# Two graph layers on one core: denominators taken up later, moved tiles and sums by ones re-dealt in the encoder, and another order at both ends of layer 1

## The chip, the cores and the metric

The kernel runs on one core of a Trainium2 chip. The metric is the device time of one execution in microseconds (us), and the median of three runs is given. The engines are PE (TensorE), ACT (ScalarE), DVE (VectorE), POOL (GpSimd) and SP (SyncE); PEld is the weight load of PE. Each works through its own instructions in order and waits for others by semaphores.

## The reference

4096 nodes with 512 features (4 heads of 128) and one adjacency `adj` of 4096 x 4096 (about 1% ones). Everything is float32.

```python
h = relu(layernorm(x)); x = x + layer0(h, adj); h = relu(layernorm(x)); x = x + layer1(h, adj)

# layer 0, per head: encoder attention, MLP, decoder attention with the same weights, MLP
Xw = h_head @ W;  f1, f2 = Xw . v1, Xw . v2
att = softmax over neighbours of sigmoid(f1_i + f2_j)
Xn = batchnorm(concat(att @ Xw))
emb = batchnorm(elu(Xn @ Wenc.T + b) + Xn)
Y = elu(concat((att @ emb_head) @ W.T))
out = batchnorm(elu(Y @ Wdec.T + b) + Y)

# layer 1, per head
feats = h @ W;  logits = leaky_relu(e_s_i + e_n_j, 0.2), neighbours only
out = relu(concat(softmax(logits) @ feats) + b)
```

## The kernel before, in words

All features lie transposed: partitions are features, columns are nodes. Five tiles `R` of 128 x 4096 hold one head each, or values of layer 1.

**Start.** Eight blocks of 512 nodes are loaded, normalized (statistics on DVE, three of four normalizations on DVE, the fourth on POOL), transposed on PE and multiplied with the heads' weights. Beside it POOL issues eight transfers (`copy_adjacency`, L446) that convert the adjacency from float32 to bytes in HBM, 1024 x 2048 each. Seven are issued here, the eighth in block 1 of the encoder (L545).

**Attention (L209 to L407)** is used three times: encoder, decoder, layer 1. Its outer loop runs over 8 blocks: 4 heads by 2 halves of 2048 target nodes. The inner loop has 32 steps j, one for each 128 source nodes. A step makes one tile `e` of 128 x 2048 weights: in the encoder and decoder two passes on ACT (L415 tanh, L416 exp) and one on DVE (L417, times the byte mask `a`, which SP loads); in layer 1 one pass on ACT (L785) and one on DVE (L786). Then PE multiplies it with the values in four products of 128 x 512 (L347), each in two instructions. Weight tiles come from rings of buffers: 8 in all in the encoder, 9 in layer 1. Every fifth tile of the encoder is stored by ACT's queue (L334) and loaded again in the decoder.

**Denominators.** The sums of the weights over all sources are made in three ways, listed by step in `ENC_FIRST`, `ENC` and `GAT` (L62 to L64) as a pair (moved, by ones). A *moved* tile is added by a DMA that POOL issues, into `acc2` or `w` (L359); each waits for the one before it. A tile *by ones* is multiplied with a block of ones on PE (L299) into one PSUM bank, `den`, which is the only one of its pool. All others are added by DVE into `acc` (L365, L367). At the end of a block PE adds both accumulators into `den` by ones.

**What follows a block** is done in the steps of the next one. `at(j, f)` puts a function at step j. At step 2 (`EVICT`) `ending` (L267) runs: ACT copies `den` to `dsb` (L246), POOL stores it and reads it back as a column `dcol` (L247, L249), and the four outputs are copied out of PSUM (DVE in the encoder L510, ACT in the others L621, L791). At step 7 DVE inverts the column (`invert_them`) and POOL stores the reciprocals `rinvs`. At steps 8, 9, 14 and 15 POOL spreads a piece over all partitions (`rb`, two buffers, L260), and five and six steps later the finishing functions run: times `rb` and statistics in the encoder (L514, L517), times `rb` and ELU in the decoder, times `rb`, ReLU and an accumulating store in layer 1 (L795, L798, L804). The decoder has no denominators of its own and reads the encoder's reciprocals. The last block of a stage finishes at once.

A scheduler builds each engine's order from the order in the code and its own estimates; `tc.issue_after(i)` and `pinned` put instructions behind a given one.

**Between.** `mlp_block` (L549) multiplies, applies ELU, adds the input and takes batch-norm coefficients (`bn_coefs`, L162) for each of four feature blocks. The decoder's MLP calls `residual` for the blocks already normalized. Layer 1 begins with the small products of `w1x` (L688, L689), then for each 512 nodes `centred` (mean by PE L700, difference L703, square L706, ReLU L707, sum of squares L708) and `deviation`; products with `w1x` follow (L731), scaled by ACT on the way out (L736). Before its attention the maximum of the scores is taken, exponentials are made, one row of terms is stored (`store_rows`, L771), and `ssum` is formed from `vacc` (L775, L776).

Of the kernel before, what the change touches and what calls it, by code (L numbers as in the profile page):

```python
# [31 lines left out]
FP = mybir.dt.float32  # L32
# [8 lines left out]
IB = 512  # L41
# [17 lines left out]
G_MAX = 75.0  # L59


ENC_FIRST = (), (4, 5, 10, 11, 15, 16, 20, 21, 25, 26, 30, 31)  # L62
ENC = (0, 3, 6, 9, 12, 15, 18, 21, 24), (4, 5, 13, 14, 30, 31)
GAT = (0, 2, 5, 7, 10, 12, 15, 17, 20, 22, 25), (9, 30, 31)  # L64

KEEP = 5
# [1 line left out]
EP = 2  # L68

EVICT = 2  # L70


VECS = [
# [6 lines left out]
def kernel(ctx, tc, x, xT, adjT, w0, w0T, v0, wencT, wdecT, vecs, w1, w1T, a1, outT):  # L80
# [12 lines left out]
    def nodes(r, ib):  # L93
        return r[:, ib * IB:(ib + 1) * IB]
# [4 lines left out]
    def bank():  # L99
        return psum.tile([P, IB], FP, name="ps")  # L100
# [13 lines left out]
    def vec_of(name):  # L114
        return vec[:, VECS.index(name), :]
# [46 lines left out]
    def bn_coefs(st, gamma, beta, a, b, lo, hi):  # L162

        mv = consts.tile([P, C, 2], FP, name="bmv", bufs=2)
        for fb in range(lo, hi):
            nc.vector.bn_aggr(mv[:, fb, :], st[:, fb].rearrange("p c s -> p (c s)"))
        a, b, mv = a[:, lo:hi], b[:, lo:hi], mv[:, lo:hi]
        rsqrt(a, mv[:, :, 1], BN_EPS)
        nc.vector.tensor_mul(a, a, vec_of(gamma)[:, lo:hi])
        nc.vector.tensor_mul(b, mv[:, :, 0], a)  # L170
        nc.vector.tensor_sub(b, vec_of(beta)[:, lo:hi], b)

    def heads_of(pv):

# [34 lines left out]
    def attention(what, keep, pools, weights, values, row_of, out, finish, ebufs, modes=None, invert=None,  # L209
# [53 lines left out]
        def at(j, f, *args):  # L263

            later.setdefault(j, []).append(lambda: f(*args))

        def ending(h, tb, po, den):  # L267

            dcol = denominators(h, tb, den) if den is not None else None
            outs = [out(spool, h, tb, s, po[s]) for s in range(SB)]  # L270
            if dcol is not None:
                at(EVICT + 5, invert_them, h, tb, dcol)
            rbs = {}
            for s, o in enumerate(outs):

                j = EVICT + 6 + s % 2 + s // 2 * 6
                at(j, lambda s=s: rbs.update({s: spread(h, tb, s)}))
                for k, f in enumerate(finish):
                    at(j + 5 + k, lambda f=f, s=s, o=o: f(spool, h, tb, s, o, rbs[s], False))

        def next_row_of(h, tb):
            rowb = keep.tile([P, TB], FP, name="rowb", bufs=2)
# [139 lines left out]
    with tc.tile_pool(name="keep", bufs=1) as keep:  # L422

        with tc.tile_pool(name="f_small", bufs=1) as small, tc.tile_pool(name="f_work", bufs=2) as work:
# [26 lines left out]
            for ib in range(NIB):  # L451
                st = work.tile([P, C, 6], FP, name="st")
                mv = work.tile([P, C, 2], FP, name="mv")
                for c in range(C):
                    nc.vector.bn_stats(st[:, c, :], xs[ib][:, c, :])
                for c in range(C):
                    nc.vector.bn_aggr(mv[:, c, :], st[:, c, :])
                rstd = work.tile([P, C], FP, name="rstd")
                last_dve = rsqrt(rstd, mv[:, :, 1], LN_EPS)
                hT = work.tile([P, C, IB], FP, name="hT")  # L460
                for c in range(C):
                    by_pool = c == C - 1
                    hn = work.tile([P, F], FP, name="hn", tag="hnp" if by_pool else "hn")
                    made = (nc.gpsimd if by_pool else nc.vector).tensor_scalar(
                        hn, xs[ib][:, c, :], mv[:, c, 0:1], rstd[:, c:c + 1], ALU.subtract, ALU.mult)

                    if by_pool and ib > 0:
                        with tc.issue_after(made.ins):
                            copy_adjacency(ib - 1, half_loaded)
                    pt = bank().rearrange("p (f n) -> p f n", n=P)  # L470
                    for fb in range(C):
                        last_pe = nc.tensor.transpose(pt[:, fb, :], hn[:, fb * P:(fb + 1) * P], ident)
                    last_act = nc.scalar.activation(hT[:, :, c * P:(c + 1) * P], pt, AF.Relu)
                if ib == 0:

                    pw = bank1()
                    with tc.issue_after(last_pe.ins):
                        for h in range(H):
                            nc.tensor.matmul(pw[:, 2 * h:2 * h + 2], w0Ts[:, h, :], v0s[:, h, :],
                                             start=True, stop=True)  # L480
                    pwh = pw[:, 0:2 * H].rearrange("p (h s) -> p h s", s=2)
                    with tc.issue_after(last_dve.ins):
                        nc.vector.tensor_copy(w0x[:, :, D], pwh[:, :, 0])
                        nc.vector.tensor_scalar_mul(w0x[:, :, D + 1], pwh[:, :, 1], 0.5)
                for c in range(C):
                    j = ib * C + c
                    for k in range(2):
                        pv = heads_of(bank())
                        for h in range(2):
                            nc.tensor.matmul(pv[:, h, :], hT[:, 2 * k + h, c * P:(c + 1) * P], w0x[:, 2 * k + h, :],  # L490
                                             start=True, stop=True)
                            nc.scalar.copy(block(R[2 * k + h], j), pv[:, h, 0:D])
                        nc.vector.tensor_copy(scores_of(j, k), pv[:, :, D:DX])
                if ib == SB - 1:
                    store_rows(rows[0], targets(0))
                    row0 = keep.tile([P, TB], FP, name="rowb", bufs=2)
                    row0_load = load_row(row0, rows[0], 0)
                    with tc.issue_after(row0_load.ins):
# [40 lines left out]
        with tc.tile_pool(name="enc", bufs=1) as spool:  # L539

            with tc.issue_after(last_act.ins), tc.issue_after(masks0[-1][1].ins):
                attention("enc", keep, spool, tanh_weights, R[0:4], lambda h, tb: (rows[tb], h), out_enc,
                          (scaled, statistics), 6, lambda n: ENC if n > 1 else ENC_FIRST, (TINY, ALU.max), "write",
                          row0=row0, masks0=masks0,
                          extras={(1, 12): lambda load: copy_adjacency(7, load),  # L545
                                  (2, 8): encoder_weights, (H * NTB - 1, NJ // 2): three_heads})


        def mlp_block(work, w, src, dst, gamma, beta, scale, between, early=None):  # L549
# [10 lines left out]
            for o in range(C):  # L560
# [7 lines left out]
                for ib in range(NIB):  # L568
# [18 lines left out]
                bn_coefs(stats, gamma, beta, a_mlp, b_mlp, o, o + 1)  # L587
# [50 lines left out]
    with tc.tile_pool(name="l_small", bufs=1) as small, tc.tile_pool(name="l_work", bufs=2) as work:  # L638
# [31 lines left out]
        def between(o, ib):  # L670
# [3 lines left out]
            elif o == C - 1 and ib >= NIB // 2:  # L674
                residual(o - 1, ib - NIB // 2)

        mlp_block(work, w, xd, x1, "dec_mlp_bn_gamma", "dec_mlp_bn_beta", None,
                  between)


# [4 lines left out]
        for fb in range(C):  # L685
            for h in range(H):
                k = 2 * (fb * H + h)
                nc.tensor.matmul(pw[:, k:k + 2], w1Ts[:, h, fb * P:(fb + 1) * P], a1s[:, h, :], start=True, stop=True)  # L688
        nc.vector.tensor_copy(w1x[:, :, :, D:DX], pw[:, 0:2 * C * H].rearrange("p (c h s) -> p c h s", h=H, s=2))  # L689
# [4 lines left out]
        def centred(ib):  # L694

            if ib >= NIB // 2:
                residual(C - 2, ib)
            residual(C - 1, ib)
            pm = bank()
            nc.tensor.matmul(pm, mean_of, S[ib], start=True, stop=True)  # L700
            hT = work.tile([P, C, IB], FP, name="hT")
            for fb in range(C):
                nc.vector.tensor_sub(hT[:, fb, :], nodes(x1[fb], ib), pm)  # L703
            sq = work.tile([P, C, IB], FP, name="sq", bufs=1)
            for fb in range(C):
                nc.scalar.activation(sq[:, fb, :], hT[:, fb, :], AF.Square)  # L706
                nc.scalar.activation(hT[:, fb, :], hT[:, fb, :], AF.Relu)  # L707
            nc.vector.tensor_reduce(S[ib], sq.rearrange("p c n -> p n c"), AX.X, ALU.add)  # L708
            return hT

# [47 lines left out]
        pm = bank1()  # L758
        nc.tensor.matmul(pm[:, 0:H], ones[0:H, :], mdiag, start=True, stop=True)
        nc.vector.tensor_copy(mbc, pm[:, 0:H])  # L760
        mb = mbc.unsqueeze(1).unsqueeze(3).to_broadcast([P, NTB, H, NJ // NTB])
        nc.vector.tensor_sub(jcol, score[:, 1], mb)
        nc.scalar.activation(jcol2, jcol, AF.Exp, scale=0.2)
# [95 lines left out]
```

## Time and profile before

| | |
|---|---|
| median of 3 runs | 3348.62 us (3343.92 to 3349.3) |
| profiled execution | 3349.09 us, its span 3347.3 us |
| granted PE clock | 0.99 |
| start, before the first full step | 0 to about 78 us |
| encoder attention, blocks 0 to 7 | about 78 to 1101 us |
| encoder MLP, decoder weights | about 1101 to 1250 us |
| decoder attention | about 1250 to 2138 us |
| decoder MLP | about 2138 to 2250 us |
| layer 1 features | about 2250 to 2399 us |
| layer 1 attention | about 2399 to 3347 us |
| DMA | 545.97 MB, 163 GB/s on average |

The profile is one execution; its times count from the first instruction. A line of the timeline gives start, duration, engine, line of the kernel, operation, output from input with shapes, and how many instructions are merged. What stands in brackets is how long the engine was idle before it and who released it. A line of the waits gives the waiting group, its releaser, the total in us, the times and the longest. "Landing" of a DMA is the time from its issue until its semaphore tells that all has arrived.

### The profile page before, as it was taken

The numbers are of one execution on the slowest core, as the hardware profiler recorded it, in microseconds if no ns is written. First come the engines' busy times: TensorE is split into PE (matmuls) and PEld (weight loads), VectorE is DVE, ScalarE is ACT, GpSimd is POOL, SyncE is SP. The second block draws the span as 40 slices with busy tenths as digits, with TensorE's granted clock in tenths as the row PEclk, the third lists the DMA queues.
The fourth block names the chain that finished last, engine by engine and source line by source line (L and its number), as shares of the span: only waits on it lengthen the run. The fifth ranks groups of instructions, "written<-read, shape, count | busy, mean of one in ns | idle before, by whom it ended". The sixth has DMA issues, their size and how long they took to land.

```text
span 3347.3 us, 26017 instructions
## 1 busy us (share of the span) xinstructions
PE 3239.2 (97%) x8943; PEld 1490.7 (45%) x8943; DVE 2679.2 (80%) x1912; ACT 2599.7 (78%) x1908; POOL 321.9 (10%) x466
## 2 busy tenths in 40 slices
PE   7998999999999999999999999999899999999999
PEld 6333434433434464444444444448644444444443
DVE  6898889889889765556665666586599999999999
ACT  7988899999999438999999999566656665665554
POOL 2000100100100000000000000024201111101110
PEclk9999999999999999999999999999999999999999
DMA  9984867867867003434443443232288789878876
GB/s 204 195 169 142 231 188 220 228 185 222 231 192 197 28 32 123 144 120 148 142 147 114 150 151 123 75 119 90 72 203 208 187 203 217 200 178 194 217 179 156
DMA packets 178437, 545.97 MB, mean 163 GB/s; under 512 B 20164, under 2 KB 23492, under 8 KB 144000
## 3 DMA queue, kind: packets, MB, share of 16 engines
q0 software_dynamic: 41360, 197.51, 30.7%
q1 hardware_dynamic: 126288, 293.66, 25.8%
q10 hardware_dynamic: 10656, 53.15, 3.9%
q8 instruction: 70, 1.15, 0.1%
q14 instruction: 63, 0.52, 0.0%
HBM read 378.15 MB, written 95.82 MB: 142 GB/s over the span
## 4 chain that ended last, share of the span: by engine, by line
PE 46%; DVE 24%; issue 12%; ACT 9%; DMA 8%; DVEq 0%; ACTq 0%; POOL 0%; POOLq 0%
PE ps L347 31%; DVE e L786 8%; PE ps L557 7%; DVE e L417 6%; DVE R L367 6%; ACT e L415 5%; PE ps L731 3%; DMA w<-e 3%; ACT e L416 3%; DVE acc L367 2%; DMA rb<-rinvs 2%; DMA a<-mask 2%; PE den L299 1%; PE ps L490 1%; PE ps L612 1%
## 5 line engine op out<-in xcount | busy, mean ns | idle before, releaser
L347 PE MATMUL ps<-e,R 128*128 128x512 f32 x6048 | 2643.6, 597 | 71.9 <-DVE e L417 54.9
L347 PEld LDWEIGHTS ps<-e,R 128*128 128x128 f32 x6048 | 1144.0, 191 | 1562.7 <-issue 1405.0
L417 DVE TENSOR_TENSOR e<-e,a 128x2048 f32<-128x2048 f32 (+1 forms) x470 | 1052.6, 2260 | 426.0 <-ACT e L416 404.1
L415 ACT ACTIVATE e<-rowb,score 128x2048 f32<-128x2048 f32 (+1 forms) x470 | 912.7, 1968 | 95.2 <-PE ps L347 59.0
L416 ACT ACTIVATE e<-e 128x2048 f32<-128x2048 f32 (+1 forms) x470 | 871.4, 1880 | 16.4 <-DVE e L417 10.0
L785 ACT ACTIVATE e<-rowb,nq,jcol 128x2048 f32<-128x2048 f32 x224 | 455.9, 2085 | 196.3 <-DMA w<-e 110.8
L786 DVE SCALAR_TENSOR_TENSOR e<-e,jcol,a 128x2048 f32<-128x2048 f32 (+1 forms) x259 | 590.6, 2317 | 3.7 <-ACT e L785 3.7
L367 DVE TENSOR_TENSOR R<-R,e 128x2048 f32<-128x2048 f32 x128 | 291.6, 2278 | 0.0
L367 DVE TENSOR_TENSOR acc<-acc,e 128x2048 f32<-128x2048 f32 x126 | 287.9, 2285 | 2.1
L557 PE MATMUL ps<-R,w 128*128 128x512 f32 x512 | 220.3, 592 | 0.6 <-DVE w L524 0.6
L260 POOL DMA_DIRECT2D rb<-rinvs x88 | 54.6, 652 | 1135.2 <-DVE R L514 834.5
L557 PEld LDWEIGHTS ps<-R,w 128*128 128x128 f32 x512 | 97.2, 190 | 122.7 <-issue 117.7
L359 POOL DMA_DIRECT2D w<-e x77 | 64.9, 843 | 620.7 <-DVE e L786 255.5
L731 PE MATMUL ps<-w1x,hT 128*128 128x260 f32 x512 | 117.8, 389 | 2.8 <-ACT hT L707 2.8
L577 ACT ACTIVATE ex<-ps,bias 128x512 f32<-128x512 f32 x64 | 44.0, 687 | 95.6 <-PE ps L557 78.5
L798 ACT ACTIVATE R<-R,vec 128x512 f32<-128x512 f32 x32 | 23.1, 720 | 117.3 <-DVE R L795 116.8
L731 PEld LDWEIGHTS ps<-w1x,hT 128*128 128x128 f32 x512 | 97.9, 193 | 22.8 <-ACT hT L707 4.4
L359 POOL DMA_DIRECT2D acc<-e x54 | 45.7, 846 | 635.5 <-DVE e L417 340.0
L785 ACT ACTIVATE e<-w,nq,jcol 128x2048 f32<-128x2048 f32 (+1 forms) x35 | 65.5, 1937 | 31.6 <-DMA dacc<-e 29.0
L299 PE MATMUL den<-e,ones 128*32 128x512 f32 x680 | 82.5, 599 | 0.0
L579 DVE SCALAR_TENSOR_TENSOR ex<-ex,re 128x512 f32<-128x512 f32 x64 | 44.9, 701 | 35.7 <-ACT re L578 35.7
L736 ACT ACTIVATE R<-ps,rstd 128x128 f32<-128x128 f32 x128 | 38.5, 366 | 40.4 <-PE ps L731 39.5
(158 smaller groups left out, 1269.8 us busy)
## 6 DMA issues: line engine op xcount, KB each, us to landing
a<-mask SPq DMA_DIRECT2D x720, 256.0 KB, 3.2
w<-e POOLq DMA_DIRECT2D x77, 1024.0 KB, 8.1
acc<-e POOLq DMA_DIRECT2D x54, 1024.0 KB, 8.5
ekeep<-e ACTq DMA_DIRECT2D x48, 1024.0 KB, 8.5
e<-ekeep SPq DMA_DIRECT2D x48, 1024.0 KB, 4.8
rb<-rinvs POOLq DMA_DIRECT2D x88, 256.0 KB, 5.2
mask<-in_adjT POOLq DMA_DIRECT2D x8, 2048.0 KB, 75.2
rowb<-rows SPq DMA_DIRECT2D x16, 1024.0 KB, 6.5
```

Of the source, the lines that this page charges most:

```text
L260: nc.gpsimd.dma_start(rb, everywhere(rinvs[h][tb], 0, s * IB, IB))
L299: last_ones = nc.tensor.matmul(den[s * 32:(s + 1) * 32, :], ones[:, 0:32], t[:, s * IB:(s + 1) * IB], start=not begun, stop=stop)
L347: last_main = nc.tensor.matmul(b, block(values[h], j), e[:, s * IB:(s + 1) * IB], start=(j == 0), stop=(j == NJ - 1))
L359: nc.gpsimd.dma_start(sums2 if n else dacc, e, **({"accum_op": ALU.add} if j > moved[0] else {}))
L367: nc.vector.tensor_add(acc, acc, e)
L415: nc.scalar.activation(e, rowb, AF.Tanh, bias=column(score[:, 1], j, h), scale=0.5)
L416: last_act = nc.scalar.activation(e, e, AF.Exp, scale=0.5)
L417: last_dve = nc.vector.tensor_mul(e, e, a)
L557: nc.tensor.matmul(z, w[:, fb, o * P:(o + 1) * P], nodes(src[fb], ib), start=(fb == 0), stop=(fb == C - 1))
L731: nc.tensor.matmul(b[:, 0:2 * DX], hT[:, fb, c * P:(c + 1) * P], w1x[:, fb, 2 * k:2 * k + 2, :].rearrange("p h x -> p (h x)"), start=(fb = ...
L785: last_act = nc.scalar.activation(e, rowb, AF.Relu, bias=column(nq, j, h), scale=column(jcol, j, h))
L786: last_dve = nc.vector.scalar_tensor_tensor(e, e, column(jcol2, j, h), a, ALU.add, ALU.mult)
```

## The change

The copy of `den`, its store and its column move from step 2 to step 4 (`INVERT`), while the outputs are still evicted at step 2. The inversion moves from step 7 to 10, the spreading from 8, 9, 14, 15 to 11, 12, 18, 19, and the finishing functions follow six and seven steps after. The lists change: the encoder's blocks 2 to 7 have eleven moved tiles (nine before) and four by ones (six before); its first two blocks keep twelve by ones, the first pair one step later. The eighth conversion of the adjacency is issued at the start, behind the seventh. At the start the statistics of the second 512 nodes stand behind the normalizations of the first. At the entry of layer 1 the copy of `w1x`'s added columns stands behind the last coefficients of the MLP; the difference is written to `sq`, ReLU reads it there, and the square is taken in place. Before layer 1's attention the sums for `ssum` stand ahead of the exponentials, and the row is stored after them.

```diff
-ENC_FIRST = (), (4, 5, 10, 11, 15, 16, 20, 21, 25, 26, 30, 31)
-ENC = (0, 3, 6, 9, 12, 15, 18, 21, 24), (4, 5, 13, 14, 30, 31)
+ENC_FIRST = (), (5, 6, 10, 11, 15, 16, 20, 21, 25, 26, 30, 31)
+ENC = (0, 2, 5, 7, 10, 12, 15, 17, 20, 22, 25), (8, 9, 30, 31)
 GAT = (0, 2, 5, 7, 10, 12, 15, 17, 20, 22, 25), (9, 30, 31)
...
 EVICT = 2
+INVERT = 4
...
-            dcol = denominators(h, tb, den) if den is not None else None
             outs = [out(spool, h, tb, s, po[s]) for s in range(SB)]
-            if dcol is not None:
-                at(EVICT + 5, invert_them, h, tb, dcol)
+            if den is not None:
+                def invert_later():
+                    dcol = denominators(h, tb, den)
+                    at(INVERT + 6, invert_them, h, tb, dcol)
+
+                at(INVERT, invert_later)
...
-                j = EVICT + 6 + s % 2 + s // 2 * 6
+                j = INVERT + 7 + s % 2 + s // 2 * 7
                 at(j, lambda s=s: rbs.update({s: spread(h, tb, s)}))
                 for k, f in enumerate(finish):
-                    at(j + 5 + k, lambda f=f, s=s, o=o: f(spool, h, tb, s, o, rbs[s], False))
+                    at(j + 6 + k, lambda f=f, s=s, o=o: f(spool, h, tb, s, o, rbs[s], False))
...
-                for c in range(C):
-                    nc.vector.bn_stats(st[:, c, :], xs[ib][:, c, :])
+
+                with pinned([first_hn] if ib == 1 else []):
+                    for c in range(C):
+                        nc.vector.bn_stats(st[:, c, :], xs[ib][:, c, :])
...
+                    if ib == 0 and not by_pool:
+                        first_hn = made
...
                             copy_adjacency(ib - 1, half_loaded)
+                            if ib == NIB - 1:
+                                copy_adjacency(ib, half_loaded)
...
-                          extras={(1, 12): lambda load: copy_adjacency(7, load),
-                                  (2, 8): encoder_weights, (H * NTB - 1, NJ // 2): three_heads})
+                          extras={(2, 8): encoder_weights, (H * NTB - 1, NJ // 2): three_heads})
...
-        nc.vector.tensor_copy(w1x[:, :, :, D:DX], pw[:, 0:2 * C * H].rearrange("p (c h s) -> p c h s", h=H, s=2))
+        with tc.issue_after(last_coefs.ins):
+            nc.vector.tensor_copy(w1x[:, :, :, D:DX], pw[:, 0:2 * C * H].rearrange("p (c h s) -> p c h s", h=H, s=2))
...
+            sq = work.tile([P, C, IB], FP, name="sq", bufs=1)
+            for fb in range(C):
+                nc.vector.tensor_sub(sq[:, fb, :], nodes(x1[fb], ib), pm)
             hT = work.tile([P, C, IB], FP, name="hT")
             for fb in range(C):
-                nc.vector.tensor_sub(hT[:, fb, :], nodes(x1[fb], ib), pm)
-            sq = work.tile([P, C, IB], FP, name="sq", bufs=1)
+                nc.scalar.activation(hT[:, fb, :], sq[:, fb, :], AF.Relu)
             for fb in range(C):
-                nc.scalar.activation(sq[:, fb, :], hT[:, fb, :], AF.Square)
-                nc.scalar.activation(hT[:, fb, :], hT[:, fb, :], AF.Relu)
+                nc.scalar.activation(sq[:, fb, :], sq[:, fb, :], AF.Square)
...
+        pss = bank1()
+        for h in range(H):
+            last_sum = nc.tensor.matmul(pss[:, h:h + 1], vacc[:, h, :], ones[:, 0:1], start=True, stop=True)
+        nc.vector.tensor_scalar_mul(ssum, pss[:, 0:H], TINY)
         mb = mbc.unsqueeze(1).unsqueeze(3).to_broadcast([P, NTB, H, NJ // NTB])
...
-        store_rows(rowsg, g.rearrange("p t h q -> p (t h q)"))
-
-        pss = bank1()
-        for h in range(H):
-            nc.tensor.matmul(pss[:, h:h + 1], vacc[:, h, :], ones[:, 0:1], start=True, stop=True)
-        nc.vector.tensor_scalar_mul(ssum, pss[:, 0:H], TINY)
+        with tc.issue_after(last_sum.ins):
+            store_rows(rowsg, g.rearrange("p t h q -> p (t h q)"))
```

More of the change, by code (lines that the diff above doesn't have):

```diff
@@ L170, in bn_coefs @@
         nc.vector.tensor_mul(b, mv[:, :, 0], a)
-        nc.vector.tensor_sub(b, vec_of(beta)[:, lo:hi], b)
+        return nc.vector.tensor_sub(b, vec_of(beta)[:, lo:hi], b)
     def heads_of(pv):
@@ L586, in mlp_block @@
                     between(o, ib)
-                bn_coefs(stats, gamma, beta, a_mlp, b_mlp, o, o + 1)
+                last = bn_coefs(stats, gamma, beta, a_mlp, b_mlp, o, o + 1)
+            return last
         with tc.tile_pool(name="m_small", bufs=1) as small, tc.tile_pool(name="m_work", bufs=3) as work:
@@ L675, in between @@
                 residual(o - 1, ib - NIB // 2)
-        mlp_block(work, w, xd, x1, "dec_mlp_bn_gamma", "dec_mlp_bn_beta", None,
+        last_coefs = mlp_block(work, w, xd, x1, "dec_mlp_bn_gamma", "dec_mlp_bn_beta", None,
                   between)
```

## The prediction

> **What bounds the kernel now.** First the busy shares and the span. TensorE looks full, but only the decoder (1250 to 2140 us) runs at its pace: 109.87 us a block of 256 products. The list of waits (us in total, times, longest) shows what stands in front of the others.
>
> ```profile
> span 3347.3 us, 26017 instructions
> PE 3239.2 (97%) x8943; PEld 1490.7 (45%) x8943; DVE 2679.2 (80%) x1912; ACT 2599.7 (78%) x1908; POOL 321.9 (10%) x466
> ```
>
> ```profile
> ACT dsb L246 <- PE den L299: 44.9, 7, 11.2
> ...
> DVE R L795 <- DMA rb<-rinvs: 29.5, 6, 6.7
> ...
> DVE R L514 <- DMA rb<-rinvs: 13.0, 3, 11.9
> ```
>
> Then the timelines of single engines give each wait its place. In the **encoder** ScalarE binds:
>
> ```profile
> 714.03 3.88 ACT L415 ACTIVATE e<-rowb,score 128x2048 f32<-128x2048 f32 x2
> 722.86 0.58 ACT L246 COPY dsb<-den 128x512 f32<-128x512 f32 x1 [4.94 <-PE den L299]
> 723.34 3.71 ACT L416 ACTIVATE e<-e 128x2048 f32<-128x2048 f32 x2
> ```
>
> Its copy of the denominators waits 4.94 us for TensorE's sums, with two exponentials behind it. In the stretch 594.9 to 719.2 ACT is busy 119.22 of 124.3 us: the wait is nearly all its idle time. In the **second encoder block**:
>
> ```profile
> 233.50 0.78 POOL L446 DMA_DIRECT2D mask<-in_adjT  x1
> 234.97 1.08 POOL L260 DMA_DIRECT2D rb<-rinvs  x2 [0.69 <-DMA rinvs<-dcol]
> ...
> 264.53 0.69 DVE L514 TENSOR_TENSOR R<-R,rb 128x512 f32<-128x512 f32 x1 [11.86 <-DMA rb<-rinvs]
> ```
>
> The reciprocals stand in Pool's queue behind the 8th conversion of the adjacency and land 29.6 us after their issue; VectorE stands 11.86 us. In **layer 1's attention** VectorE stops each block for the same kind of transfer:
>
> ```profile
> 3024.97 0.69 DVE L795 TENSOR_TENSOR R<-R,rb 128x512 f32<-128x512 f32 x1 [6.66 <-DMA rb<-rinvs]
> 3143.72 0.69 DVE L795 TENSOR_TENSOR R<-R,rb 128x512 f32<-128x512 f32 x1 [6.23 <-DMA rb<-rinvs]
> ```
>
> TensorE is near its floor there (109.87 plus five sums of 0.905 = 114.4 us). From the timeline of TensorE the blocks end 114.8, 114.9, 115.4, 117.0, 119.1, 118.7 us apart. At the **entry of layer 1** a copy stands in front of the last MLP step:
>
> ```profile
> 2251.63 0.19 DVE L689 COPY w1x<-den 128x32 f32<-128x32 f32 x1 [2.29 <-PE den L688]
> ```
>
> **What the Trainium skill says.** "PSUM — Partial Sum Buffer", Engine vs sequencer instructions: the queues of ScalarE, VectorE and GpSimd are strict FIFO. The trace agrees: the exponentials start at 723.34, after the copy. "DMA: Bandwidth & Descriptors", Issuing engines are not separate DMA queues: transfers of all issuers interleave on the same 16 engines. The trace agrees: stores of kept weights land in 4 to 5 us alone and 9 to 11 beside an accumulation, which takes 10 to 11 instead of about 8. "Perfetto Trace Analysis", Identifying the Most-Contended Engine: matmul busy share is a poor measure for TensorE; here it is 97% while blocks differ by 15 us.
>
> **The change, part by part.** Orders are those of the two built programs. The base is the profiled execution: 3349.1 us, span 3347.3 plus 1.8 around it; the median is 0.5 lower.
>
> *1. Denominators later, encoder blocks 2 to 7.* In ScalarE's built order the copy passes not two steps but two exponentials (1.80 us each, 3.60). The wait before, as a sum: DVE's last idle time is at tile 15 (773.44). From there to tile 30 it has 16 masks of 2.21, 11 adds of 2.255, 4 small operations of 0.605, together 62.5; then 0.35 for hand-overs, two tiles of products (6.87) and four sums (3.62): 73.4. ACT has 19 tanh of 1.895 and 18 exponentials of 1.80, 68.4. The difference, 4.95, is the traced 4.94. After: multiplying and statistics move from tiles 12-20 to 16-25, so more lies after DVE's last idle, now tile 13: 18 masks, 12 adds, 8 small ones, 71.6, plus 10.84, against 21 tanh and 22 exponentials, 79.4. That leaves 3.0 of wait: 1.9 less a block, six blocks, **-11.4**. Bounds: the wait wholly gone, -29; nothing, 0. Two sums less on TensorE (1.8 us a block) lie under ScalarE; they would count only if TensorE were late. VectorE's adds stay at 16. What is late next is the same copy.
>
> *2. Eleven moved tiles.* Two more accumulations a block are issued by Pool. Each waits for the one before; Pool's other issues wait behind. They hold their tile until they land; ACT asks for the same buffer 8 tiles later, some 29.6 us. A tile is masked 6 to 14 us after ACT starts it, a landing takes 4.5/8.5/12.6 us (min/median/max), so a backlog of some 5 us is covered. Moved tiles now come every 2.5 tiles of 3.73, 9.3 us, close to the mean landing of 9.5 (without the first of a block). I take 0; bounds -0.5 a block (DMA tails) and the first rival.
>
> *3. Eighth conversion at once, block 1.* The 11.86 wait goes, and 1.3 of small VectorE idles (0.57, 0.69) with ScalarE's earlier release. But the seventh conversion lands at 212.0 (issue 55.8 plus 156.2), the eighth then some 27 to 30 later, 239 to 242, and now the denominators queue behind it: two small transfers of about 3.2 each less overlap, 245. VectorE is at the inversion about 242.5 (208.5, four copies 2.4, six adds 13.5, eight masks 17.7, plus gaps): 2.5 lost. Mask loads in that stretch share the engines: VectorE lost 1.75, 1.28 and 1.43 between 183 and 206; I take 1.5. **-9**; bounds -13 and -4.
>
> *4. Start.* The third normalization no longer waits behind two statistics that wait for their input (2.24 idle); TensorE's gap of 2.78 shrinks. Block 0 is then paced by mask loads that land in 15 to 22 us, so little of it lasts: **-1**, bounds -2.7 and +0.5.
>
> *5. Entry of layer 1.* The copy goes behind the coefficients: -2.2 (the 2.29 wait). ReLU before squares brings the first weights forward, and the sums of squares come 1 us later: **-3** together, bounds -4.5 and -1.5. *Exit:* ssum's wait moves ahead of the row's store; ScalarE lost 2.53 to it, but VectorE now waits 1.8 for the sum before the row's terms; 0, bounds -1 and +1.6.
>
> *6. Layer 1's attention.* ScalarE's and Pool's order around the denominators is the same as before; only the first multiplication moves from after tile 13 to after tile 16: three masks of 2.27 and two adds of 2.25, 11.3 us later, more than the longest wait of 6.7. The waits go; TensorE gets back 0.6+2.2+4.3+3.9 over 114.8, and about 1 in the last block: **-12**. VectorE's idle 29.5 isn't the gain, since TensorE's queue covered the rest. Next late: TensorE itself. Bounds -13 and -4 (third and fourth reciprocals now behind more accumulations).
>
> *7. Decoder.* Its finishing steps and the order of kept-weight loads move, but TensorE idles 2.6 of 890 us: 0; if the cover went, one late step of 3.4 a block.
>
> Sum: 11.4+9+1+3+12 = 36.4, so 3349.1-36.4 = **3312.7**.
>
> **Rivals.** *Tiles held by moved sums.* For it: layer 1 has the same positions, and ACT waits there 110.8 us for such landings; it has slack, the encoder has none. Against: 9.5 is just within. At landings of 10.1 the seven accumulations after tile 10 fall 5 us behind by tile 22, ACT waits 4 to 5 a block, 3.0 of which the copy's wait gives back: the 11.4 are gone and a few us more. 3313+15 = 3328.
> *Slower.* The same queue as the bound: ten accumulations a block make each further us of landing cost 8 to 10. It decides when a block takes 129, 7 us over my 121.8 (6 x 7 = 43 eats the 36.4 and 6.7 more), at landings near 11; at 11.3, 131: 3368. Against: accumulations follow one another, so two more don't overlap; mean landings in layer 1, at 80% DMA share, are 8.4.
> *The wait goes wholly.* -29 for -11.4: 3295. Against: the sum in 1.
> *Reciprocals late again in layer 1*: gain 4 instead of 12: 3321.
> *Nothing comes of it*: the waits return one step later: 3345.
>
> **How the numbers follow.** Likeliest 0.56; tiles held 0.17; wholly gone 0.12; late reciprocals 0.08; slower 0.04; nothing 0.03. A difference of 0.2% (6.7 us) is about what can be told from none. Faster 0.93, same 0.03, slower 0.04. The range 3297 to 3336 takes in the likeliest, late reciprocals, most of the tiles held and half of the wholly gone.
>
> **What would show it.** ACT's wait at the copy near 3 us, encoder blocks 122 apart; ACT waiting for accumulations in the encoder speaks for the first rival. No VectorE wait on reciprocals in layer 1, blocks 114.8 apart; block 1 near 129 with a short wait at the inversion; the products of layer 1 three us earlier after the MLP. I am wrong if encoder blocks stay at 124 or VectorE waits for reciprocals.

## The result and the profile after

| | before | after |
|---|---|---|
| median | 3347.14 us (3343.92 to 3349.3, 4 runs) | 3310.01 us (3307.08 to 3313.2, 4 runs) |
| profiled execution, its span | 3347.3 us | 3308.6 us |

The change makes the kernel faster: ratio 0.989, 95% interval 0.9873 to 0.9907. The forecast was 3312.7. The profiled spans differ by 38.7 us; each stage's share comes from TensorE's timelines. A block is counted from the end of TensorE's sums of one block to that of the next, the decoder MLP from its first product.

| stage | forecast | measured |
|---|---|---|
| start and encoder block 0 | -1 | -5.4 |
| encoder block 1 (137.87, then 133.15) | -9 | -4.7 |
| encoder blocks 2 to 7 (752.3, then 733.4) | -11.4 | -18.9 |
| encoder MLP and decoder | 0 | -1.7 |
| decoder MLP to layer 1's first sums (382.63, then 381.95) | -3 | -0.7 |
| layer 1's attention from there (826.6, then 819.2) | -12 | -7.4 |
| sum | -36.4 | -38.7 |

The total was met, its terms were not: two were too small, three too large, and the decoder's is scatter (see below). First two lines of the page of the kernel after, then its list of waits (us in total, times, longest).

```profile
span 3308.6 us, 25868 instructions
...
PE 3226.6 (98%) x8847; PEld 1492.2 (45%) x8847; DVE 2677.1 (81%) x1912; ACT 2602.9 (79%) x1908; POOL 329.1 (10%) x478
```

```profile
ACT dsb L247 <- PE den L303: 19.6, 7, 5.2
...
DVE R L808 <- DMA rb<-rinvs: 14.3, 4, 8.7
...
DVE dcol L254 <- DMA dcol<-dens: 6.3, 1, 6.3
...
DVE R L524 <- DMA rb<-rinvs: 1.1, 2, 0.8
```

Busy times have hardly moved: what went are waits. The copy's 44.9 became 19.6, layer 1's 29.5 became 14.3, the 13.0 at L514 (11.86 of them in the second encoder block) became 1.1, and one is new, for `dcol`. Steady blocks of the encoder show it, one before and then two neighbours after (us, then busy time and instructions of PE, PEld, DVE, ACT and POOL, then granted clock, DMA share, GB/s):

```profile
722.79:846.87 124.08, 118.94 (x322) 49.75 (x321) 114.23 (x62) 119.22 (x65) 11.54 (x17) 1.00 0.75 212
```

```profile
701.76:823.86 122.10, 118.39 (x305) 50.09 (x305) 115.61 (x63) 119.22 (x65) 13.18 (x19) 0.99 0.85 233
823.86:944.68 120.82, 118.39 (x305) 50.05 (x305) 113.20 (x65) 119.21 (x65) 13.16 (x19) 0.99 0.89 244
```

ScalarE is busy for the same 119.22 us; its idle time shrinks. From its timeline after:

```profile
817.48 3.70 ACT L420 ACTIVATE e<-e 128x2048 f32<-128x2048 f32 x2
823.92 0.59 ACT L247 COPY dsb<-den 128x512 f32<-128x512 f32 x1 [2.75 <-PE den L303]
824.41 3.90 ACT L419 ACTIVATE e<-rowb,score 128x2048 f32<-128x2048 f32 x2
```

The wait is 2.75 where it was 4.94. It alternates with 1.48 from block to block, and so does the order that the scheduler built for VectorE at the end of a block. Blocks 2 to 6 are 120.8, 122.1, 120.8, 122.1 and 120.8 apart. In the second encoder block (block 1), from the timelines of Pool, VectorE and TensorE:

```profile
206.08 0.59 POOL L248 DMA_DIRECT2D dens<-dsb  x1 [151.85 <-ACT dsb L247]
241.84 0.59 POOL L250 DMA_DIRECT2D dcol<-dens  x1 [35.17 <-DMA dens<-dsb]
```

```profile
244.26 0.17 DVE L254 TENSOR_SCALAR dcol<-dcol 128x16 f32<-128x16 f32 x1 [6.30 <-DMA dcol<-dens]
```

```profile
239.61 3.60 PE L351 MATMUL ps<-e,R 128*128 128x512 f32 x8
249.00 9.43 PE L351 MATMUL ps<-e,R 128*128 128x512 f32 x16 [5.79 <-DVE e L421]
```

An 8 KB store stands 35 us behind the 8th conversion, which landed at 240.8. VectorE stands 6.30 us for the column that depends on the store, and TensorE 5.79 us for VectorE. In layer 1 VectorE still waits four times for reciprocals, the longest time in the third block:

```profile
2657.27 0.69 DVE L808 TENSOR_TENSOR R<-R,rb 128x512 f32<-128x512 f32 x1 [8.73 <-DMA rb<-rinvs]
```

That block takes 118.88 and the fourth 115.54 (its wait is 3.05). The other full ones take 114.83 and the last 111.39. At the entry of layer 1 the copy follows the coefficients without a wait:

```profile
2222.37 0.16 DVE L172 TENSOR_TENSOR coefs<-vec,coefs 128x1 f32<-128x1 f32 x1
2222.45 0.18 DVE L700 COPY w1x<-den 128x32 f32<-128x32 f32 x1
```

### The profile page after: what moved, and what is told of

Same layout as the page of the kernel before. It is cut to its first block, busy times and chain, and to the rows that moved or that the text cites. A ratio compares the mean times of both kernels' runs of the same rounds, so it can differ in the third digit from the quotient of the medians.

```text
span 3308.6 us, 25868 instructions
## 1 busy us (share of the span) xinstructions
PE 3226.6 (98%) x8847; PEld 1492.2 (45%) x8847; DVE 2677.1 (81%) x1912; ACT 2602.9 (79%) x1908; POOL 329.1 (10%) x478
## 4 chain that ended last, share of the span: by engine, by line
PE 67%; DVE 16%; issue 9%; ACT 5%; DMA 3%; DVEq 0%; ACTq 0%; POOL 0%; POOLq 0%
PE ps L351 52%; PE ps L566 7%; DVE e L421 4%; DVE e L799 4%; DVE R L371 4%; PE ps L743 3%; ACT e L419 2%; PE den L303 2%; DVE acc L371 2%; ACT e L420 2%; DMA a<-mask 2%; PE ps L622 1%; PE ps L348 1%; PE ps L500 1%; DMA rb<-rinvs 1%
## 5 line engine op out<-in xcount | busy, mean ns | idle before, releaser
L363 POOL DMA_DIRECT2D w<-e x77 | 64.6, 839 | 643.6 <-DMA w<-e 267.5
L743 PE MATMUL ps<-w1x,hT 128*128 128x260 f32 x512 | 119.6, 393 | 1.8 <-ACT hT L717 1.8
L363 POOL DMA_DIRECT2D acc<-e x66 | 55.6, 842 | 607.7 <-DMA acc<-e 225.7
L588 DVE SCALAR_TENSOR_TENSOR ex<-ex,re 128x512 f32<-128x512 f32 x64 | 45.0, 703 | 35.7 <-ACT re L587 35.5
L303 PE MATMUL den<-e,ones 128*32 128x512 f32 x584 | 70.9, 599 | 0.0
```

Of the source, the lines that this page charges most:

```text
L303: last_ones = nc.tensor.matmul(den[s * 32:(s + 1) * 32, :], ones[:, 0:32], t[:, s * IB:(s + 1) * IB], start=not begun, stop=stop)
L363: nc.gpsimd.dma_start(sums2 if n else dacc, e, **({"accum_op": ALU.add} if j > moved[0] else {}))
L743: nc.tensor.matmul(b[:, 0:2 * DX], hT[:, fb, c * P:(c + 1) * P], w1x[:, fb, 2 * k:2 * k + 2, :].rearrange("p h x -> p (h x)"), start=(fb = ...
```

## The experiments

The ratio is to the kernel before, timed beside each. "Theory" is what I held before a run, after the traces that I had by then; "rival" is the other account. Several theories fell.

| kernel | median us | ratio to before (95%) |
|---|---|---|
| later_alone | 3317.07 | 0.9905 (0.9889 to 0.9922) |
| lists_alone | 3347.83 | 0.9995 (0.9987 to 1.0004) |
| lists_old | 3315.08 | 0.9896 (0.9882 to 0.9909) |
| cast_back | 3306.2 | 0.987 (0.9856 to 0.9883) |
| cols_other_queue | 3301.08 | 0.9852 (0.9839 to 0.9866) |
| start_old | 3307.47 | 0.9876 (0.986 to 0.9891) |
| gat_inv5 | 3304.92 | 0.9862 (0.9848 to 0.9875) |
| edges_old | 3311.91 | 0.9883 (0.987 to 0.9897) |
| enc_inv6 | 3294.19 | 0.9835 (0.9821 to 0.9848) |
| moved14 | 3355.33 | 1.0019 (1.0011 to 1.0028) |
| best | 3288.04 | 0.982 (0.9806 to 0.9833) |
| best_start_old | 3290.8 | 0.9827 (0.9813 to 0.984) |

### later_alone: the main part alone

Against the kernel before; it also has the new `ending`:

```diff
-ENC_FIRST = (), (4, 5, 10, 11, 15, 16, 20, 21, 25, 26, 30, 31)
-ENC = (0, 3, 6, 9, 12, 15, 18, 21, 24), (4, 5, 13, 14, 30, 31)
+ENC_FIRST = (), (5, 6, 10, 11, 15, 16, 20, 21, 25, 26, 30, 31)
+ENC = (0, 3, 6, 9, 12, 15, 18, 21, 24), (7, 8, 13, 14, 30, 31)
...
+INVERT = 4
```

> The kernel before with the main part alone: denominators taken up two steps later (the sums by ones of steps 4 and 5 become 7 and 8, in the first blocks 5 and 6, so that they come after the copy); nine moved tiles, conversion, start and edges of layer 1 as before. Theory: this part carries most of the gain: encoder blocks 2 to 7 as in the run with the old lists (11.4 us less than before), block 1 near 130 us (8 less, as with the conversion at step 12), layer 1's attention 7 us less, with one wait of 8 us left in its third block; together 26 us, about 3322. Rival: the parts depend on each other, and without the new lists, the early conversion or the new edges it gains less than 17 us: above 3331.

Measured: 3317.07, and a span 31.8 us under that of before, out of the whole change's 38.7. Block 1 took 130.41, blocks 2 to 7 740.9 (-11.4). The theory holds; the gain is 5 us more than expected. Of these, 2 come from an earlier end of block 0, 1.8 from the decoder and layer 1's features (equal code scatters as much, see below), and 2 from layer 1's attention, 9.1 for 7. There the long block (117.88) was the fourth and not the third. VectorE waits for reciprocals in it (in the third it waits 4.67, and that block isn't longer):

```profile
2779.78 0.69 DVE L799 TENSOR_TENSOR R<-R,rb 128x512 f32<-128x512 f32 x1 [5.47 <-DMA rb<-rinvs]
```

In block 1 of the encoder VectorE still waits 5.99 for reciprocals behind the 8th conversion, but TensorE is no longer idle for more than 1.9 us at a time, and its granted clock is 1.00 throughout. In the kernel before it stood idle for 8.73 us at this place, and its next sixteen product instructions took 9.94 us, where sixteen take 7.13 elsewhere:

```profile
269.68 9.94 PE L347 MATMUL ps<-e,R 128*128 128x512 f32 x16 [8.73 <-DVE e L417]
```

### lists_old and lists_alone: the lists taken back, and alone

In lists_old, against the kernel after, and in lists_alone, against the kernel before:

```diff
-ENC = (0, 2, 5, 7, 10, 12, 15, 17, 20, 22, 25), (8, 9, 30, 31)
+ENC = (0, 3, 6, 9, 12, 15, 18, 21, 24), (7, 8, 13, 14, 30, 31)
```

```diff
-ENC = (0, 3, 6, 9, 12, 15, 18, 21, 24), (4, 5, 13, 14, 30, 31)
+ENC = (0, 2, 5, 7, 10, 12, 15, 17, 20, 22, 25), (8, 9, 30, 31)
```

> The changed kernel with nine moved tiles and six sums by ones in the encoder as before (steps 4 and 5 of these become 7 and 8, behind the later copy of the denominators). Theory: the later copy alone brings the encoder's gain, the new lists nothing; blocks 2 to 7 stay at 121 to 122 us apart, the copy waits 1.5 to 3 us, and the time is within 3 us of 3310. Rival: the lists bring what the gain is above my 11.4 us (7.7 us); then the blocks are near 122.8 apart and the time near 3318.

> The kernel before with nothing but the encoder's new list: eleven moved tiles, four sums by ones. Theory: ScalarE's wait at the copy of the denominators stays near 4.9 us, because the sums that TensorE loses lie under ScalarE; blocks 3 to 6 stay 124.1 to 124.7 us apart and the time is within 3 us of 3347. Rival: the two sums fewer (1.8 us a block) count, the wait falls to about 3.1, blocks are 122.4 apart and the time is near 3336. Other rival: the added accumulations hold tiles, ScalarE waits for them, and the time rises above 3352.

Alone, the lists bring nothing: blocks 2 to 7 sum to 752.7 (before 752.3); blocks 2 to 6 are about 1 us longer each, block 7 is 4.1 shorter. The time is as the theory had it, though the copy waits more and not the same: 5.8 to 5.9 us a block, where it was 4.7 to 5.3; and VectorE waits 1.2 to 1.6 us for reciprocals in four of the six blocks, which it does not in the kernel before. Taken back from the changed kernel, the lists cost 7.5 us in blocks 2 to 7 (740.9 against 733.4). There my theory fell, and the rival was right as to the amount (7.7), though not as to the place: blocks 2 to 6 are 121.5 and 122.75 in turn, not 122.8. With the old lists the copy waits 0.65 more in every one of these (ScalarE):

```profile
826.83 0.59 ACT L247 COPY dsb<-den 128x512 f32<-128x512 f32 x1 [3.40 <-PE den L303]
```

Five such blocks make 3.3; the other 4.25 are in block 7 (130.97 against 126.72). There VectorE stands idle 16.4 us up to the small bias step (L541) with the old lists and 12.3 with the new ones; the largest single wait is that of the bias step itself, for a product of TensorE, 5.87 against 3.82. So in the last block TensorE's lateness seems to count. Which part of the 4.25 is the two sums and which the order around them, these runs don't separate. Why the copy gains 0.65 in the others was not traced.

### cast_back and cols_other_queue: block 1

In cast_back, and then in cols_other_queue, where `store` and `load` are those of ScalarE and SP for the denominators of block 0 alone:

```diff
-                            if ib == NIB - 1:
-                                copy_adjacency(ib, half_loaded)
...
+                          extras={(1, 12): lambda load: copy_adjacency(7, load),
```

```diff
-            nc.gpsimd.dma_start(dens[h][tb], dsb[0:P:32, :])
+            store(dens[h][tb], dsb[0:P:32, :])
...
-            nc.gpsimd.dma_start(dcol, dens[h][tb].rearrange("s (q k) -> (s q) k", k=TB // P))
+            load(dcol, dens[h][tb].rearrange("s (q k) -> (s q) k", k=TB // P))
...
+            if what == "enc" and (h, tb) == (0, 0):
+                return nc.scalar.dma_start, nc.sync.dma_start
```

> The changed kernel with one part undone: the 8th conversion is issued at step 12 of encoder block 1 again, with the denominators still taken up two steps later. Theory: issued at the start, this conversion is what the small transfers of block 1 stand behind (VectorE's 6.30 us wait for dcol). At step 12 it starts at about 233 us and lands near 262, the reciprocals then near 268, and the first multiplication now comes only at step 17, near 272: no wait is left, block 1 shrinks from 133.15 to about 128 us and the whole time from 3310 to about 3305. Rival (my prediction's step 3): moving the conversion is what takes the 11.86 us wait away, so with it back VectorE waits for rb by some 8 us again and the time is near 3316.

> The changed kernel with one edit: in encoder block 1 the store of the denominators goes through ScalarE's queue and the load of their column through SP's queue, no longer through Pool's behind the 8th conversion. Theory: TensorE is the bound of block 1 (256 products and 13 sums, nothing to catch up with), so VectorE's wait of 6.30 us for the column is paid in full as TensorE's idle 5.79 us; without it block 1 shrinks from 133.15 to about 127.5 us and the time from 3310 to about 3304.5. Rival: the wait is covered, as in other blocks, by slack of TensorE, or something else of the 8th conversion (mask loads, reciprocals behind it) takes its place; block 1 stays above 131.5.

With the conversion back at step 12 VectorE waits for `rb` again, as the rival had it:

```profile
269.84 0.69 DVE L522 TENSOR_TENSOR R<-R,rb 128x512 f32<-128x512 f32 x1 [6.53 <-DMA rb<-rinvs]
```

but TensorE's pieces of idle time are now 2 us and less, block 1 takes 129.93 and not 133.15, and the time isn't longer. The rival was right about the wait, the theory about the time. Block 1 ends at 336.5 (338.0 in the kernel after; 337.1 and 337.4 in two others with the same block 1), so bringing the conversion forward gained nothing here and may have cost a little: the later denominators alone had already taken TensorE's long idle piece away, as later_alone shows. With the two small transfers on other queues the column lands at 231.7, while the conversion still runs (to 237.6), and there is no wait at the inversion. Block 1 in the kernel after and in this one (columns as above):

```profile
204.86:338.01 133.15, 125.87 (x362) 51.64 (x361) 124.84 (x70) 119.32 (x65) 4.42 (x8) 0.97 0.59 161
```

```profile
206.31:331.23 124.92, 123.74 (x362) 50.67 (x361) 123.29 (x68) 119.44 (x65) 3.33 (x6) 1.00 0.63 170
```

Block 1 gains 8.2 us for a wait of 6.30: more than the theory's 5.6. TensorE is the bound here (123.7 of 124.9 busy), so its idle time is paid in full, and something more: in the kernel after it runs at a lower clock once it starts again (same columns):

```profile
236.00:243.00 7.00, 7.00 (x17) 2.85 (x15) 1.97 (x1) 6.97 (x4) 0.59 (x1) 1.00 0.90 299
...
249.00:256.00 7.00, 7.00 (x11) 3.10 (x12) 6.96 (x4) 7.00 (x4) 1.08 (x2) 0.67 0.65 187
```

```profile
246.80:253.60 6.80, 4.61 (x6) 2.02 (x7) 6.76 (x4) 6.80 (x4) 1.63 (x3) 0.50 0.49 144
```

Sixteen product instructions take 9.43 after the idle time and 7.13 elsewhere: 2.3 us. The Trainium skill has this in "TensorE: Matmul & The Clock Gate", Part 1: The HAM clock gate (the "warmup" mystery): after an idle window of about 3.4 us the array runs at half its clock until it has been busy for such a window. The trace agrees: the granted clock is 0.50 from 246.8 to 253.6, so it falls 3.6 us into the 5.79 us of idle time and comes back 4.6 us after TensorE starts again.

### start_old: the start

```diff
-                with pinned([first_hn] if ib == 1 else []):
+                with nullcontext():
```

> The changed kernel with one part undone: the statistics of the second input block are no longer put behind the third normalization of the first. Theory (from the two traces): the encoder's block 0 takes over the whole gain of the start, so its sums end near 209 us instead of 204.9, and everything after shifts by 4 us: about 3314. Rival (my prediction's step 4): block 0 is paced by the mask loads, so its sums end within 1.5 us of 204.9 and the time is 3310 to 3311.

Block 0's sums end at 208.65, as the theory said, yet the time doesn't rise: the span is 4.3 us shorter, with block 1 at 125.01 against 133.15. The 8th conversion lands at 237.4 (240.8 in the kernel after), and not later because block 0 is; VectorE waits 1.64 for `dcol` and not 6.30, and TensorE's gap is 1.14. The theory that the start's gain lasts to the end fell, and so did the rival as to block 0. The start itself differs between runs of equal code: VectorE's first masking begins at 64.6 to 67.8 us in nine profiles with the pin (mean 66.3) and at 67.2 to 69.8 in five without (mean 68.4). The pin is worth about 2 by these means. That before and after differ by 5.4 at the end of block 0 is partly the draw: 3.1 stand at the first masking already, and 2.3 come inside block 0, whose length differs as much between kernels with the same start.

### gat_inv5: layer 1's remaining wait

`inv_step` is 5 in layer 1 and 6 elsewhere:

```diff
-                    at(INVERT + 6, invert_them, h, tb, dcol)
+                    at(INVERT + inv_step, invert_them, h, tb, dcol)
```

> The changed kernel with one edit: in layer 1 the column of denominators is inverted one step earlier (step 9), so that Pool issues the store of the reciprocals before the accumulation of tile 10, whose issue waits 10.04 us for the one before it. Theory: that wait ahead of the reciprocals is why VectorE still stands 8.73 us for them in layer 1's third block; without it the third block shrinks from 118.88 to about 115 us, the fourth from 115.54 to 114.83, and the time from 3310 to about 3305.5. Rival: the pieces come late because accumulations share the DMA engines with them; the wait stays over 5 us and the third block over 117.5.

The theory holds: every block but the last takes 114.83, and 4.8 us are gained. What was in the way, from Pool's timeline in layer 1's third block, before, after and here:

```profile
2657.28 0.87 POOL L359 DMA_DIRECT2D w<-e  x1 [7.12 <-DMA w<-e]
2657.82 0.89 POOL L255 DMA_DIRECT2D rinvs<-dcol  x1
2667.05 1.11 POOL L260 DMA_DIRECT2D rb<-rinvs  x2 [8.34 <-DMA rinvs<-dcol]
```

```profile
2638.83 0.85 POOL L363 DMA_DIRECT2D w<-e  x1 [10.04 <-issue]
2639.37 0.88 POOL L256 DMA_DIRECT2D rinvs<-dcol  x1
2647.14 0.85 POOL L363 DMA_DIRECT2D w<-e  x1 [6.90 <-DMA w<-e]
2647.68 1.44 POOL L261 DMA_DIRECT2D rb<-rinvs  x2
```

```profile
2628.60 0.88 POOL L256 DMA_DIRECT2D rinvs<-dcol  x1
2638.63 0.84 POOL L363 DMA_DIRECT2D w<-e  x1 [9.15 <-issue]
2639.18 1.43 POOL L261 DMA_DIRECT2D rb<-rinvs  x2
```

Before, the spreads were issued 28.9 us after `dens` (2638.13), with three accumulations between; after, 41.2 us (2606.51), with five; here 32.4 (2606.74), with four. The number alone does not make the loss, though: in lists_old, whose layer 1 is the same code, Pool has the same five ahead in the third block, but the spreads come 37.0 us after `dens`, VectorE waits 5.00 and not 8.73, and the block takes 115.06. So it also counts how long the accumulations ahead take and how much work TensorE has in hand (a wait of 5.47 did lengthen the fourth block of later_alone). Why they were quicker in lists_old was not traced.

### edges_old: both ends of layer 1

```diff
-        with tc.issue_after(last_coefs.ins):
+        with nullcontext():
...
-                nc.scalar.activation(hT[:, fb, :], sq[:, fb, :], AF.Relu)
...
+                nc.scalar.activation(sq[:, fb, :], hT[:, fb, :], AF.Square)
+                nc.scalar.activation(hT[:, fb, :], hT[:, fb, :], AF.Relu)
...
-        with tc.issue_after(last_sum.ins):
-            store_rows(rowsg, g.rearrange("p t h q -> p (t h q)"))
+        store_rows(rowsg, g.rearrange("p t h q -> p (t h q)"))
```

The sums of `vacc` and `ssum` stand behind the row's store again.

> The changed kernel with both ends of layer 1 in the old order (the small copy before the last coefficients, square before ReLU, the sum of the values after the row's store). Theory (from the two traces): the 3.3 us that the first products gain are given back inside the features, so the new order is worth about 1 us up to the first denominators of layer 1, and the time stays within 2 us of 3310. Rival (my prediction's step 5): the entry's gain lasts, so layer 1's first denominators come 3 us later and the time is near 3313.

The theory holds. From the decoder MLP's first product (2107.40 in the kernel after, 2108.03 here) to layer 1's first mean (L711) it is 119.90 us with the old edges and 117.65 with the new ones: 2.25, the forecast's first part. To the first feature product it is 124.78 and 121.49: 3.29, the forecast's whole entry (TensorE, after and here):

```profile
2228.89 5.98 PE L743 MATMUL ps<-w1x,hT 128*128 128x260 f32 x16 [1.79 <-ACT hT L717]
```

```profile
2232.81 1.67 PE L742 MATMUL ps<-w1x,hT 128*128 128x260 f32 x3 [2.84 <-ACT hT L718]
```

From there on most of it is given back, and equal code scatters: to layer 1's first sums it is 382.5 to 382.8 in the four kernels with the old edges and 380.0 to 382.0 in the ten with the new ones (mean 381.3). The gain is about 1.3 of the forecast 3; by the medians alone the kernels can't be told apart.

### enc_inv6, best and best_start_old: going on

In `ending`, where all three uses of `INVERT` become `inv`; best also has the edit of gat_inv5, best_start_old that of start_old as well:

```diff
+            inv = INVERT + 2 if what == "enc" else INVERT
...
-                at(INVERT, invert_later)
+                at(inv, invert_later)
```

> The changed kernel with one edit: in the encoder the denominators are taken up at step 6, two steps later again (inversion at 12, spreads from 13 on). Theory: ScalarE's copy now passes two more exponentials (3.60 us), more than the 1.48 and 2.75 us that it still waits, so the wait goes and ScalarE is never idle: blocks 2 to 6 come down from 120.83 and 122.10 to about 119.4 us, and the time from 3310 to about 3299. Rival: TensorE or VectorE is as late as ScalarE by then, so the blocks stay above 120.5 and the time above 3306.

> The changed kernel with two edits together: the encoder takes its denominators up at step 6, and layer 1 inverts them a step earlier (step 9). Theory: the two act in different stages, so their gains add: 16.8 us of the spans for the first, 4.5 us for the second, about 3289 us; layer 1's blocks are all 114.83 apart. Rival: one spoils the other; above 3293.

> The same two edits, and the start's pin undone. Theory: undoing the pin paid 4.3 us in the changed kernel only because VectorE's wait behind the 8th conversion ended block 1's stall at a fixed time; with the inversion at step 12 that wait is gone, so now the start counts: block 0 ends some 3 to 4 us later and the time is near 3292. Rival: the start as it was is better by itself (the conversions start earlier); then the time is 3286 or less.

With the copy at step 6 it no longer waits (ScalarE), and ScalarE fills its blocks (columns as above, busy of PE, PEld, DVE, ACT, POOL):

```profile
694.92 0.56 ACT L247 COPY dsb<-den 128x512 f32<-128x512 f32 x1
```

```profile
570.87:690.21 119.34, 116.22 (x305) 49.66 (x305) 114.03 (x64) 118.63 (x66) 13.23 (x19) 1.00 0.87 238
690.21:810.16 119.95, 116.49 (x306) 49.60 (x305) 114.00 (x63) 119.66 (x66) 13.23 (x19) 1.00 0.88 237
```

Blocks 2 to 6 take 119.6 on average (118.3 to 120.9), close to the theory's 119.4, blocks 2 to 7 lose another 8.9 us, and block 1 comes to 123.74, which I had not expected: the column lands at 244.8, and VectorE comes to the inversion only at 246.7, so that it no longer waits for what stands behind the conversion. Together with the edit of layer 1 the time is 3288.04, 22 us under the changed kernel (15.8 and 5.1 alone): the two gains add. Without the pin it is 3290.8 (3290.21 to 3291.68, against 3286.21 to 3292.73), which fits the pin's 2 us, but the ranges overlap, and in the two profiles the first masking begins at the same time (67.8 and 67.7); this pair doesn't settle it.

### moved14: where Pool's queue binds

```diff
-ENC = (0, 2, 5, 7, 10, 12, 15, 17, 20, 22, 25), (8, 9, 30, 31)
+ENC = (0, 2, 4, 6, 7, 10, 12, 14, 16, 18, 20, 22, 24, 26), (8, 9, 30, 31)
```

> The changed kernel with fourteen moved tiles in the encoder's blocks 2 to 7 instead of eleven (three of VectorE's adds fewer). It measures how near the eleven are to the point where Pool's queue binds. Theory: the accumulations follow one another and land in 8.6 us beside stores and mask loads, so fourteen of them (8.6 x 14 = 120.4) fill a block of 121 us; the queue falls behind, ScalarE waits for tiles that they hold, blocks are 123 to 128 us apart and the time is 3320 to 3345. Rival: the DMA engines have room (their share was 0.85 to 0.89), landings shorten as the stores move apart; blocks stay below 121.5 and the time at or under 3310.

The slower rival's mechanism is real, at fourteen and not at eleven, and stronger than the theory of this run had it (blocks of 123 to 128): blocks 2 to 6 are 129 to 133 us apart, 46 us more over blocks 2 to 7. ScalarE waits for tiles that accumulations hold, a wait that the kernel after does not have at all:

```profile
ACT e L419 <- DMA acc<-e: 54.6, 22, 5.3
```

The landings did not grow: 8.9 us on average with nine moved tiles, 8.8 with eleven, 8.5 with fourteen. What binds is their number: each is issued after the one before has landed, and at fourteen the issues are some 9.3 us apart, which fills a block of 130 us.

## Why the prediction was right, step by step

**Right in sum, by terms that offset each other.** Start, encoder and decoder together gained 9.3 us more than forecast, layer 1 6.9 less. The main mechanism was right; that the sum came within 3 us is in good part luck.

1. *Denominators later in the encoder.* Confirmed as the main cause by later_alone (31.8 of 38.7 us, with its effect in block 1 and layer 1). The amount came too: with the old lists blocks 2 to 7 gain 11.4. It is not six times 1.9, though, so that the exact agreement is luck: 4.8 in block 2, where the wait had been longer, 1.3 to 3.2 in the middle, and block 7 loses 2.1. The wait of 3.0 that I worked out is 2.13 and 3.40 with the old lists, mean 2.8.
2. *Eleven moved tiles: 0.* The rival of held tiles is refuted at eleven: ScalarE never waits for an accumulation in the encoder, and landings stay short (8.8). What failed is "Two sums less on TensorE (1.8 us a block) lie under ScalarE": with the later copy the new lists are worth 0.65 a block and about 4 in block 7, 7.5 in all. That it is the two sums, and not the moved tiles or the order, isn't shown; and with the old, early copy the lists are worth nothing.
3. *Eighth conversion: -9.* The step that failed is "VectorE is at the inversion about 242.5". The conversion landed at 240.8 and the column at 244.2, as worked out, but VectorE came at 237.96, because block 0 had ended 5.4 earlier, and 2.5 lost became 6.30. I had set an event on the conversions' clock against one on the block's clock, and had moved neither with my own step 4. I also priced the loss on VectorE, where TensorE pays it with a restart at lower clock. The runs show that the early conversion was not needed at all.
4. *Start: -1.* By the means of the first masking it is worth about 2, within the bounds. The reason given for "little of it lasts" failed: block 0 keeps the gain (from its first masking to its sums it takes 138.4 to 140.7 in every kernel, whenever it begins). It is block 1 that returns it, to the wait for the conversion.
5. *Entry of layer 1: -3.* It came in full at the first feature product (3.29, of which 2.25 stand at the first mean already). It did not last, as the forecast took for granted: about 1.3 are left at layer 1's first sums, and most of the loss lies ahead of its first attention product.
6. *Layer 1's attention: -12.* With the wait gone it is 12.1, as gat_inv5 shows. The change got 7.4, since "ScalarE's and Pool's order around the denominators is the same as before" is false for Pool in the first blocks: two more accumulations came ahead of the spreads there (five for three). By the prediction's own sign ("I am wrong if ... VectorE waits for reciprocals") this part was wrong in the third block. The rival of late reciprocals was half true.
7. *Decoder: 0.* From its first product to the MLP's it took 887.2 us against 888.9; both values occur among kernels whose decoder is the same, so this is scatter.

## What to carry to other kernels

When a wait sits on an engine with a full queue, moving the waiting step to a later place, past the work behind it, is worth a try step by step until the wait is gone; here the second move of two steps brought 15.8 us, the side edits of the change together about 7 (38.7 less 31.8). Before pricing a move, lay down for each small transfer what is ahead of it in its own queue, and keep events of two clocks (a chain of long transfers, a chain of blocks) apart: a gain on one is lost where it meets the other. Look for the built order of every block, not of a steady one only.

## What the runs showed of the hardware

- An idle time of TensorE of 5.8 us cost 8.1 in block 1: the granted clock was 0.67 in the 7 us after it. After 8.73 us of idle time, in the kernel before, sixteen product instructions took 9.94 us and not 7.13. After pieces of 1.9 us and less, in cast_back and later_alone, the clock stayed at 1.00.
- An 8 KB store issued by Pool behind an 8 MB conversion took 35.5 us to land. In all nine kernels where it stands behind the conversion it landed less than 1 us after it, though it was issued at 205.0 to 213.2; sent through ScalarE's queue, with its column through SP's, it did not wait for the conversion.
- More accumulating transfers of 1 MB, one after another, did not land later (8.9, 8.8 and 8.5 us on average with nine, eleven and fourteen moved tiles a block), though the DMA share rose from 0.75 to 0.93.
- Equal code differed by up to 3 us at the start, 1.7 us in the decoder and 2 us in layer 1's features between profiles, more than some edits are worth; a stage's gain has to be read from several profiles.
